# A 3x3 depthwise convolution divided anew between TensorE and VectorE, in a kernel whose instruction order is planned

## The chip, the core and the metric

The kernel runs on one core of one Trainium2 chip. The metric is device time in microseconds (us) from the first to the last instruction with the little that lies around it; the time of the kernel before is the median of three runs. The profile is of one execution on that core.

## The reference, cut to what matters

The input is 32 images of 96 channels and 56x56 pixels, in float32. Each image goes through three parts, and the change is in the first.

```python
# part 1, the convolution block (32 images)
h = relu(bn(einsum('oc,bchw->bohw', w1, x)))      # 96 -> 576 channels
h = relu(bn(dwconv3x3(h, wdw)))                   # each channel by itself, 9 taps
x = x + bn(einsum('oc,bchw->bohw', w2, h))        # 576 -> 96 channels
# part 2, a mixer over the 3136 pixels as tokens
t = t + bn(w2 @ irfft(relu(diag * fft(relu(bn(w1 @ ln(t)))) + bias)))
# part 3, a feed-forward block with rounding to fp8 (5,2) and fp16
t = t + q(W2 @ q(relu(q(W1 @ q(ln(t)) + b1))) + b2)
```

The batch norms are folded into weights and biases when the kernel starts. The depthwise convolution of 576 channels is the largest elementwise work: nine multiply-adds for each of 576 x 3136 values of an image.

## The kernel before, in words

**Stages.** An image is cut into two halves of 28 rows (`R`). For every half, `load_half` brings 29 rows of the 96 input channels into one of three `xs` buffers. The 576 hidden channels are four groups of 128 (`k` = 0 to 3, `NK` = 4) and the last 64.

For each of the four groups, `unit(img, s, k)` does this: `expand` multiplies by `w1T` on TensorE into PSUM (L617), ScalarE evicts with bias and relu into `hs` (L627), ScalarE starts the accumulator `acc` with one tap and the bias (L643, `begin`), and VectorE adds seven taps one by one with a multiply-add over 28 rows (L670, `tap`). The ninth tap is a `product` that ScalarE makes (L659) and that a DMA with addition, issued by GpSimd, adds to `acc` (L678). The groups named in `DOUBLE` (`k` = 1 and 3) make two products, so that VectorE has six taps left; the second product is added to the first by another such DMA. At the end ScalarE applies relu to `acc` (L687).

The last 64 channels have no taps on VectorE. `last_channels` puts even and odd rows on the two halves of the 128 partitions (`hl`, evicted at L738 and L742), and TensorE does the nine taps as matmuls with matrices of diagonals (`band`, L755): of a half image, 12 matmuls with a stationary operand of 128x64 and 12 of 64x64. ScalarE evicts the sum with bias and relu (L784, `al`).

`front` then multiplies the 576 channels by `w2T`, pixel rows becoming partitions (L883 for the four groups, L920 for the last 64), adds the input (a transpose in the same accumulation), evicts (L933), and runs the norm and the first part of the mixer. `mid` does the rest of the mixer, for two halves of the spectrum, and `back` the inverse transform and the feed-forward block, for four quarters.

**Order.** Nothing of this is emitted in the order in which it is written. Every piece is a `step` with an engine, an estimated cost, what it comes after, buffers that it takes and gives, and a rank. `Plan.emit` plays the steps through and gives each engine, whenever it is idle in that play, the ready step of lowest rank. Work of several images so stands interleaved on each engine, and each engine runs its own list strictly in order. Where TensorE has little to do in that play, the planner places `filler` matmuls (L1491), which compute nothing that is used.

**PSUM** is three buffers of two banks for everything (`ps`), and one of two banks for the accumulation of `front` (`pw`), in which the filler also has a corner.

Of the kernel before, what the change touches and what calls it, by code (L numbers as in the profile page):

```python
# [41 lines left out]
C = 96  # L42
# [12 lines left out]
NK = 4  # L55
G = 7
# [71 lines left out]
START = {"last": 9, "front": 7, "mid": 62, "back": 98}  # L128
PACE = {"last": 3.023, "front": 0.4, "mid": 0.54, "back": 0.45}
# [6 lines left out]
SPARSE = 0.75  # L136
FILLER = 0.23
FIRST = 15.0
# [4 lines left out]
DOUBLE = (1, 3)  # L143
# [15 lines left out]
class Plan:  # L159
# [12 lines left out]
    def __init__(self, free):  # L172
        self.free = dict(free)
        self.steps = []
        self.now = self.pace = 0.0
        self.window, self.share, self.slow = 0, {}, False
        self.moving = 0.0
        self.filler, self.recent = None, []
# [20 lines left out]
    def sparse(self, now):  # L199

        self.recent = [r for r in self.recent if r[1] > now - self.WINDOW]
        return sum(b - max(a, now - self.WINDOW) for a, b in self.recent) < SPARSE * self.WINDOW

# [10 lines left out]
    def step(self, engine, cost, emit, after=(), take=(), give=(), late=None, rank=None):  # L214
        late = self.LATE.get(engine, 0.1) if late is None else late
        if rank is None:
            rank = self.now
            self.now += self.pace
        s = Step(engine, cost, emit, list(after), list(take), list(give), late, rank, len(self.steps))
        self.steps.append(s)  # L220
        return s

    def emit(self):
# [6 lines left out]
        work = sum(s.engine == "PE" for s in self.steps)  # L230
        while events:
# [12 lines left out]
            for engine, heap in ready.items():  # L244
# [3 lines left out]
                while heap:  # L248
# [13 lines left out]
                    if engine == "PE":  # L262
                        self.recent.append((now, now + cost))
                        work -= 1
# [7 lines left out]
                if engine == "PE" and idle[engine] and work and now > FIRST and self.sparse(now):  # L272

                    self.filler()
                    idle[engine] = False
                    cost = self.stretched(now, FILLER)
                    self.recent.append((now, now + cost))
                    heapq.heappush(events, (now + cost, count, engine, None))
                    count += 1
# [4 lines left out]
def tile_kernel(ctx: ExitStack, tc: tile.TileContext, d: dict, out: bass.AP):  # L284
# [5 lines left out]
    psa = ctx.enter_context(tc.tile_pool(name="psa", bufs=3, space=PSUM))  # L290
    psw = ctx.enter_context(tc.tile_pool(name="psw", bufs=1, space=PSUM))
    dram = ctx.enter_context(tc.tile_pool(name="scratch", bufs=2, space=DRAM))


    pw = psw.tile([128, 2, 512], F32, name="pw", tag="pw")
# [25 lines left out]
    w1T = cst([C, HD], "w1T")  # L321
# [12 lines left out]
    b1 = cst([128, NK + 1], "b1")  # L334
# [10 lines left out]
    band = cst([128, 2, 3, 128], "band")  # L345
    gd = cst([KD, G, C], "gd")
    xnT = cst([C + 1, G, 128], "xnT")
    xs_ring = [cst([C, XW], f"xs{j}") for j in range(3)]


    hl = [cst([128, RP + 1, S], f"hl{s}") for s in range(2)]


    scratch = [w1.tile([128, G * SK], F32, name="eo", tag="brief", bufs=8) for _ in range(3)]
    scratch += [w1.tile([128, G * SK], F32, name="V", tag="brief", bufs=8) for _ in range(2)]
# [26 lines left out]
    load(nc.sync, w1T, d["w1T"])  # L382
# [5 lines left out]
    nc.gpsimd.memset(band, 0.0)  # L388
    nc.gpsimd.memset(hl[0][0:64, 0, :], 0.0)
    nc.gpsimd.memset(hl[1][64:128, RP, :], 0.0)  # L390
    nc.gpsimd.memset(ones, 1.0)

    def loads():
# [3 lines left out]
        for s in range(2):  # L397
            load(q, w2T[64 * s : 64 * s + 64, NK, :], d["w2T"][NK * 128 :, :])
        yield rows
# [46 lines left out]
    for k in range(NK + 1):  # L446
# [7 lines left out]
        )  # L454
    shift_of(b1, vec[:, 1, :], vec[:, 2, :], s, tmp(128, NK + 1))
    nc.vector.tensor_mul(w1T[:, 0:512], w1T[:, 0:512], ps[0:C, 0, :])
    nc.vector.tensor_mul(w1T[:, 512:HD], w1T[:, 512:HD], ps[0:C, 1, 0 : HD - 512])
# [5 lines left out]
    def bands(j):  # L463
        def f():

            for dc in range(3):
                for i in range(2):
                    for o in range(2):
                        dr = 2 * j - 1 + i - o
                        if abs(dr) <= 1:  # L470
                            at, to = slice(64 * i, 64 * i + 64), slice(64 * o, 64 * o + 64)
                            k = 3 * (dr + 1) + dc
                            nc.vector.tensor_scalar_mul(band[at, j, dc, to], ident[at, at], wdw[at, NK, k : k + 1])

        return f

    def second():
# [11 lines left out]
        nc.vector.tensor_mul(w2T, w2T, s.unsqueeze(1).to_broadcast([128, NK + 1, C]))  # L489

# [38 lines left out]
    def ffn():  # L529
# [6 lines left out]
        for o, v, p, n in ((b1q, fb, 128, 3), (b2q, fc, C, 1)):  # L536
# [11 lines left out]
            "ps": 3, "pw": 1, "hs": 3, "acc": 7, "product": 3, "hl0": 1, "hl1": 1, "al": 2,  # L548
            "xt": 1, "norma": 2, "brief": 8, "xnT": 1, "z": 2, "ya": 1, "wb": 1, "yb": 2,
# [21 lines left out]
    bands_set = [step("DVE", 1.2, bands(j), rank=2.0 + j) for j in range(2)]  # L571
    sets = []
    for n, (f, count) in enumerate(((second, 7), (attention, 6), (mixer, 21), (ffn, 4))):
        t = step("SP", 0.55 * count, fetch, sets[-1:], late=(150e3, HARD), rank=-20.0 + n)
        sets.append(step("DVE", 3.0, f, sets[-1:] + [t], rank=14.0 + 4 * n))
    second_set, mixer_set, *mid_set = sets

    def spare(name, p, n):

        t = w1.tile([128, R, S], F32, name=name, bufs={"acc": 7, "product": 3}[name])  # L580
# [5 lines left out]
    def load_half(img, s):  # L586
# [8 lines left out]
        if n >= 3:  # L595
            i, t = divmod(n - 3, 2)
            after = [taken[i, t], strips[i, t, "hl"]]
        loaded[img, s] = step("SP", 0.1, load, after, late=read(C * XW), rank=16 * n - 24)

    def unit(img, s, k):  # L600
        n = (2 * img + s) * NK + k
        o = R * s - base[s]
        up = 1 - 2 * s
# [6 lines left out]
        def expand(h):  # L610
            def mm():
                if h == 0:
                    u["hs"] = w2.tile([128, XR, S], F32, name="hs", bufs=3)
                u[h] = psum()
                for j in range(2):
# [4 lines left out]
                        rhs=xs[img, s][0:C, at : at + QW],  # L620
# [4 lines left out]
            def evict():  # L625
                flat = u["hs"].rearrange("p r c -> p (r c)")
                nc.scalar.activation(  # L627
                    flat[:, 2 * h * QW : 2 * (h + 1) * QW].rearrange("p (j w) -> p j w", j=2),
                    u[h][:, :, 0:QW],
                    AF.Relu,  # L630
                    bias=b1[:, k : k + 1],
                )

            after = [loaded[img, s]] if h == 0 else [u["first"]]
            e = u["first"] = step("PE", pe(QW, 128, 4), mm, after, ["ps"] + ["hs"] * (h == 0), rank=4 * n + OFF[0] + h)
            return step("ACT", act(2 * QW, 1), evict, [e], [], ["ps"], rank=4 * n + OFF[0] + h)

        e = [expand(0), expand(1)]

        def begin():  # L640

            acc[img, s, k] = w1.tile([128, R, S], F32, name="acc", bufs=7)
            nc.scalar.activation(  # L643
                acc[img, s, k],
                u["hs"][:, o + up : o + up + R, :],
# [5 lines left out]
        def span(dr, dc):  # L651

            return max(0, -(o + dr)), min(R, XR - o - dr), max(0, -dc), S - max(0, dc)

        def product(dr):
            def f():
                ra, rb, _, _ = span(dr, 0)
                u["p", dr] = w1.tile([128, R, S], F32, name="product", bufs=3)
                nc.scalar.activation(  # L659
                    u["p", dr][:, ra:rb, :], u["hs"][:, ra + o + dr : rb + o + dr, :], AF.Copy, scale=weight(dr, 0)  # L660
# [4 lines left out]
        def tap(dr, dc):  # L665
            def f():
                ra, rb, ca, cb = span(dr, dc)
                src = u["hs"][:, ra + o + dr : rb + o + dr, ca + dc : cb + dc]
                dst = acc[img, s, k][:, ra:rb, ca:cb]
                nc.vector.scalar_tensor_tensor(dst, src, weight(dr, dc), dst, ALU.mult, ALU.add)  # L670
# [888 lines left out]
```

## Time and profile before

| | |
|---|---|
| median of three runs | 4469.97 us (4468.09 to 4476.27) |
| profiled execution, span | 4469.5 us |
| TensorE: matmul records, busy | 34916, 98% of the span |
| VectorE: instructions, busy | 7053, 96% |
| ScalarE: instructions, busy | 5390, 92% |
| DMA engines, mean busy in the steady part | 75% |
| one image in the steady part | 134.6 us |

The time of the profiled execution is its span, 4469.5 us, and the fraction of a microsecond around it; it stands within 0.5 us of the median. The lines of the profile give, for a group of instructions, the line of the kernel, the engine, the operation, `out<-in` by the program's names, the shapes, the count, the summed busy time and the mean duration in nanoseconds, and behind a bar the idle time of the engine ahead of it and what ended it. A float32 matmul leaves two records in the trace, so that counts of TensorE's records are twice those of the program. Records of TensorE [...]overlap: the time that a run of matmuls really takes is read from the start of the run to the start of the next one, in the timeline.

### The profile page before, as it was taken

The numbers are of one execution on the slowest core, as the hardware profiler recorded it, in microseconds if no ns is written. First come the engines' busy times: TensorE is split into PE (matmuls) and PEld (weight loads), VectorE is DVE, ScalarE is ACT, GpSimd is POOL, SyncE is SP. The second block draws the span as 40 slices with busy tenths as digits, with TensorE's granted clock in tenths as the row PEclk, the third lists the DMA queues.
The fourth block names the chain that finished last, engine by engine and source line by source line (L and its number), as shares of the span: only waits on it lengthen the run. The fifth ranks groups of instructions, "written<-read, shape, count | busy, mean of one in ns | idle before, by whom it ended". The sixth has DMA issues, their size and how long they took to land.

```text
span 4469.5 us, 87997 instructions
## 1 busy us (share of the span) xinstructions
PE 4366.5 (98%) x34916; PEld 3248.3 (73%) x34916; DVE 4307.1 (96%) x7053; ACT 4103.5 (92%) x5390; POOL 339.6 (8%) x403
## 2 busy tenths in 40 slices
PE   8999999999999999999999999999999999999998
PEld 5767777777777777777777777777777777777777
DVE  8999999999999999999999999999999999999977
ACT  5778999999999999999999999999999999999975
POOL 1100000000000000000000000000000000000000
PEclk9999999999999999999999999999999999999999
DMA  5667777777777777777777777777777777777763
GB/s 106 144 147 174 192 172 184 189 176 183 192 171 188 187 176 184 189 176 184 187 173 191 187 174 188 182 176 192 184 176 188 176 180 194 180 177 191 169 180 107
DMA packets 390992, 789.43 MB, mean 177 GB/s; under 512 B 135696, under 2 KB 236628, under 8 KB 390580
## 3 DMA queue, kind: packets, MB, share of 16 engines
q1 hardware_dynamic: 335028, 479.15, 38.1%
q0 software_dynamic: 55488, 304.64, 34.2%
q8 instruction: 275, 4.51, 0.4%
q14 instruction: 137, 1.12, 0.1%
q10 hardware_dynamic: 64, 0.01, 0.0%
HBM read 286.38 MB, written 192.68 MB: 107 GB/s over the span
## 4 chain that ended last, share of the span: by engine, by line
PE 37%; DVE 32%; ACT 15%; issue 3%; DMA 3%; ACTq 0%; DVEq 0%; POOLq 0%; SPq 0%
DVE acc L670 20%; PE pw L883 10%; PE ps L617 5%; PE ps L1005 3%; PE ps L1036 3%; PE ps L1123 3%; PE ps L1329 2%; ACT h L1395 2%; DVE sb L1152 2%; DVE V L1152 2%; DMA acc<-product 2%; ACT product L659 1%; ACT hs L627 1%; PE ps L755 1%; PE ps L1447 1%
## 5 line engine op out<-in xcount | busy, mean ns | idle before, releaser
L670 DVE SCALAR_TENSOR_TENSOR acc<-hs,wdw,acc 128x1540 f32<-128x1540 f32 (+2 forms) x1664 | 2970.5, 1795 | 5.9 <-ACT acc L643 0.3
L617 PE MATMUL ps<-xs,w1T 96*128 96x406 f32 x2048 | 808.9, 517 | 27.2 <-ACT al L784 12.9
L883 PE MATMUL pw<-w2T,acc 128*112 128x96 f32 x7168 | 788.6, 264 | 3.8 <-ACT acc L687 3.7
L883 PEld LDWEIGHTS pw<-w2T,acc 128*112 128x112 f32 x7168 | 750.5, 179 | 57.5 <-issue 34.6
L659 ACT ACTIVATE product<-hs,wdw 128x1568 f32<-128x1568 f32 (+1 forms) x384 | 610.8, 1599 | 15.2 <-DMA product<-product 15.0
L617 PEld LDWEIGHTS ps<-xs,w1T 96*128 96x128 f32 x2048 | 355.6, 190 | 291.5 <-issue 165.1
L627 ACT ACTIVATE hs<-ps,b 128x812 f32<-128x812 f32 x512 | 481.3, 940 | 84.4 <-PE ps L617 79.5
L678 POOL DMA_DIRECT2D acc<-product x256 | 223.3, 872 | 3709.6 <-DVE df L855 687.2
L643 ACT ACTIVATE acc<-hs,bd,wdw 128x1568 f32<-128x1568 f32 x256 | 436.9, 1707 | 0.2
L755 PE MATMUL ps<-hl,band 128*64 128x385 f32 (+3 forms) x3072 | 418.7, 497 | 4.8 <-ACT hs L627 4.8
L687 ACT ACTIVATE acc<-acc 128x1568 f32<-128x1568 f32 x256 | 388.0, 1516 | 26.1 <-DMA acc<-product 19.9
L1005 PEld LDWEIGHTS ps<-watt,xnT 97*120 97x120 f32 x1792 | 293.2, 182 | 97.3 <-issue 40.8
L1005 PE MATMUL ps<-watt,xnT 97*120 97x192 f32 x1792 | 339.1, 330 | 19.8 <-DVE V L1152 14.7
L1123 PEld LDWEIGHTS ps<-wb,yb 112*128 112x128 f32 x3528 | 297.0, 164 | 48.1 <-issue 35.8
L1410 ACT ACTIVATE h<-h 128x784 fp8e5<-128x784 f16 x348 | 300.2, 863 | 34.4 <-DVE h L1401 34.3
L1395 ACT ACTIVATE h<-ps 128x784 f16<-128x784 f32 x384 | 317.0, 828 | 12.3 <-PE ps L1383 11.5
L1350 ACT ACTIVATE u<-tt,mf,rf 112x96 fp8e5<-112x96 f32 x812 | 317.0, 465 | 0.7
L1123 PE MATMUL ps<-wb,yb 112*128 112x112 f32 x3528 | 317.2, 269 | 0.0
L755 PEld LDWEIGHTS ps<-hl,band 128*64 128x64 f32 (+1 forms) x3072 | 152.7, 135 | 203.0 <-issue 163.4
L1401 DVE TENSOR_SCALAR h<-h,b1q 128x784 f16<-128x784 f16 x384 | 162.3, 423 | 88.9 <-ACT h L1395 88.8
L1036 PE MATMUL ps<-z,wa 56*64 56x384 f32 (+1 forms) x2048 | 223.9, 498 | 1.7 <-ACT hs L627 1.7
L1329 PE MATMUL ps<-gd,wd 114*112 114x96 f32 x1792 | 200.2, 264 | 2.3 <-DMA gd<-gdr 2.0
(171 smaller groups left out, 6621.3 us busy)
## 6 DMA issues: line engine op xcount, KB each, us to landing
acc<-product POOLq DMA_DIRECT2D x256, 784.0 KB, 8.7
product<-product POOLq DMA_DIRECT2D x128, 756.0 KB, 11.2
yb<-ydr SPq DMA_DIRECT2D x252, 294.0 KB
wd<-in_wd_dram SPq DMA_DIRECT2D x128, 349.1 KB
wb<-in_wb_dram SPq DMA_DIRECT2D x63, 686.0 KB
ydr<-ya SPq DMA_DIRECT2D x256, 168.0 KB
xs<-in_x_dram SPq DMA_DIRECT2D x64, 609.0 KB
tdr<-xt SPq DMA_DIRECT2D x64, 588.0 KB
```

The costliest lines, as they stand in the source:

```text
L617: nc.tensor.matmul(u[h][:, j, 0:QW], lhsT=w1T[:, 128 * k : 128 * (k + 1)], rhs=xs[img, s][0:C, at : at + QW], start=True, stop=True,)
L627: nc.scalar.activation(flat[:, 2 * h * QW : 2 * (h + 1) * QW].rearrange("p (j w) -> p j w", j=2), u[h][:, :, 0:QW], AF.Relu, bias=b1[:, k ...
L643: nc.scalar.activation(acc[img, s, k], u["hs"][:, o + up : o + up + R, :], AF.Identity, scale=weight(up, 0), bias=bd[:, k : k + 1],)
L659: nc.scalar.activation(u["p", dr][:, ra:rb, :], u["hs"][:, ra + o + dr : rb + o + dr, :], AF.Copy, scale=weight(dr, 0))
L670: nc.vector.scalar_tensor_tensor(dst, src, weight(dr, dc), dst, ALU.mult, ALU.add)
L687: nc.scalar.activation(acc[img, s, k], acc[img, s, k], AF.Relu)
L755: nc.tensor.matmul(pv[:, :, ca:cb], lhsT=band[rows, j, dc + 1, 64 * o : 64 * o + 64], rhs=H[rows, q : q + 7, ca + dc : cb + dc], skip_grou ...
L883: nc.tensor.matmul(u["pw"][0:SK, t, n % 4, 0:C], lhsT=src[rows, (G * t + n) * SK : (G * t + n + 1) * SK], rhs=rhs, skip_group_check=True, **k,
L1005: nc.tensor.matmul(pv[0:PK, q - a, 0:HA], lhsT=xnT[:, q, 0:PK], rhs=watt, start=True, stop=True,)
L1036: nc.tensor.matmul(u["y", b][64 * c : 64 * c + n, j, 0 : 2 * HA], lhsT=wa[at, 0:n], rhs=rhs, start=True, stop=True)
L1123: nc.tensor.matmul(o, lhsT=lhsT, rhs=u["wb"][:, G * s + q, :], start=True, stop=True)
L1395: nc.scalar.activation(u["h", c].rearrange("p (j w) -> p j w", j=2), u["H", c][:, :, 0:n], AF.Copy)
```

## The change

**Channels 384 to 511** (`k` = 3, now `QK`) leave VectorE. A new function `quads` expands them as before, and does the nine taps on TensorE: the array is used as sixteen tiles of 32x32. A half image is four windows of seven rows; for each tap there are sixteen matmuls, one for each pair of a block of 32 input channels and a window, each with a 32x32 diagonal (`wq`) as stationary operand and seven rows as moving operand. Window `t` of channel block `i` goes to output partitions `32*((i + t) % 4)` of a bank that belongs to the window, so the channels stand rotated by window, and `w2r`, `bdr` are rotated copies of weights and bias. The nine taps are three steps, the two PSUM buffers are held over all three, and ScalarE evicts them with four activations into `q_ring`.

**The last 64 channels** leave TensorE's taps. They become one `unit` for the whole image ("pair"): the two image halves lie on the two halves of the 128 partitions, even and odd rows interleaved by window, so that the taps of both are done by VectorE in instructions of the same size as those of the other groups. Two short matmuls with zeros (`nought`) fill the row beyond the image's edge.

**The rest.** `front` takes three groups from `w2T`, the rotated one from `w2r` (one more matmul per 128 columns where a tile of 112 pixels crosses two windows), and the last 64 from the pair. The bias of `expand` becomes a row of `w1T` against a row of ones in `xs`, so evictions apply relu alone. `filler` and the buffer `pw` are gone, and PSUM is four equal buffers. There are two `product` buffers in place of three. `DOUBLE` names the units (0, 1), "pair" and (1, 1). A table `NUDGE` adds a number to the rank of each step of an image.

```diff
+HS, ACCS, PRODUCTS, BRIEFS = 3, 7, 2, 8
+UNIT = 32 / 7
+ORDER = {(0, 0): 0, (0, 1): 1, (0, 2): 2, "pair": 3, (1, 0): 4, (1, 1): 5, (1, 2): 6}
+NUDGE = (-7.64, 3.75, 0.79, ...)
-DOUBLE = (1, 3)
+DOUBLE = ((0, 1), "pair", (1, 1))
...
+        if self.place is not None:
+            rank += NUDGE[self.place] if self.place < len(NUDGE) else 0.0
+            self.place += 1
...
-    psa = ctx.enter_context(tc.tile_pool(name="psa", bufs=3, space=PSUM))
-    psw = ctx.enter_context(tc.tile_pool(name="psw", bufs=1, space=PSUM))
+    psa = ctx.enter_context(tc.tile_pool(name="psa", bufs=4, space=PSUM))
...
-    def last_channels(img, s):
+    def quads(img, s):
...
+        def taps(first):
+            def f():
+                if first == 0:
+                    for n in range(2):
+                        u["d", n] = psum()
+                for dr, dc in TAPS[first : first + 3]:
+                    at = 3 * (dr + 1) + dc + 1
+                    ca, cb = max(0, -dc), S - max(0, dc)
+                    for j in range(4):
+                        for i in range(4):
+                            t = (j - i) % 4
+                            row = 7 * t + R * s - base[s] + dr
+                            ra, rb = max(0, -row), min(7, XR - row)
+                            pv = u["d", t // 2][32 * j : 32 * j + 32, t % 2, 0 : 7 * S].rearrange("p (r c) -> p r c", c=S)
+                            nc.tensor.matmul(
+                                pv[:, ra:rb, ca:cb],
+                                lhsT=wq[32 * i : 32 * i + 32, at, :],
+                                rhs=u["hs"][32 * i : 32 * i + 32, row + ra : row + rb, ca + dc : cb + dc],
+                                start=(dr == 0 and dc == 0),
+                                stop=(dr, dc) == TAPS[-1],
+                                skip_group_check=True,
+                            )
...
+                for b in range(2):
+                    at = 15 * t + 8 * b
+                    nc.scalar.activation(
+                        q_ring[n % 2][:, at : at + 7, :].rearrange("p r c -> p (r c)"),
+                        u["d", t][:, b, 0 : 7 * S],
+                        AF.Relu,
+                        bias=bdr[:, 2 * t + b : 2 * t + b + 1],
+                    )
...
-                    for k in range(NK):
+                    for k in range(QK):
...
+                    src = acc[img, (s, QK)].rearrange("p (t r) c -> p t (r c)", t=2)[:, t, :]
+                    for b in (0,) if i < 3 else (1,) if i > 3 else (0, 1):
+                        at = (2 * i + b) * S
+                        nc.tensor.matmul(
+                            u["pw", i // 4][0:SK, t, i % 4, 0:C],
+                            lhsT=src[:, at : at + SK],
+                            rhs=w2r[:, 2 * t + b, :],
...
     for i in range(nimg):
+        plan.place = 0
         for s in range(2):
             load_half(i, s)
-            last_channels(i, s)
-            for k in range(NK):
-                unit(i, s, k)
+        for s in range(2):
+            quads(i, s)
+        for what in ORDER:
+            unit(i, what)
+        for s in range(2):
             front(i, s)
```

Counted over the program, VectorE's taps go from 1664 instructions to 1472, the accumulating DMAs from 384 to 320, and TensorE's depthwise matmuls from 1536 to 9216.

## The prediction

> **What bounds the kernel now.** I read the busy shares first, then the stretches (is there a steady part, and how long is one image?), then the groups by form, and last TensorE's timeline, since its busy share is no measure.
>
> ```profile
> PE 4366.5 (98%) x34916; PEld 3248.3 (73%) x34916; DVE 4307.1 (96%) x7053; ACT 4103.5 (92%) x5390; POOL 339.6 (8%) x403
> ```
>
> Three engines look full. Two neighbouring stretches of 134.6 us (columns: stretch, length, then busy time of PE, PEld, DVE, ACT, POOL) hold the same work:
>
> ```profile
> 2000.00:2134.60 134.60, 133.16 (x1072) 98.39 (x1072) 132.26 (x215) 129.41 (x173) 10.40 (x12) 1.00 0.75 183
> 2134.60:2269.20 134.60, 132.91 (x1069) 98.18 (x1069) 132.18 (x215) 129.15 (x172) 10.41 (x12) 1.00 0.75 182
> ```
>
> So one image takes 134.6 us, and 32 of them 4307; the other 162 us of the span are the start and the end. VectorE is idle for 2.4 us of an image (1.8%): it is the bound. ScalarE needs 129.3. [...]I took its need from the timeline of 26 images (538 to 4038 us): for each kind of run (line, length, whether the next one uses the array in tiles) the fastest fifth of the times from its start to the next run's start counts as work, what others take beyond as waiting. Work comes to 130.1 us an image. In it are the filler matmuls (the stretch, their busy time and records):
>
> ```profile
> 538.40:4038.00 3499.60, 66.44 (x416) 57.66 (x416) 1.00 0.75 183
> ```
>
> A pair of their records lasts 0.22 us start to start, longer ahead of a change of mode: 2.1 us an image. **TensorE's own need is 128.0 us**, close under VectorE's. That is the number on which this prediction rests.
>
> [...]The trace shows two and four tiles at once; sixteen no run here shows:
>
> ```profile
> 2038.63 2.17 PE L755 MATMUL ps<-hl,band 128*64 128x392 f32 x12
> 2040.73 1.63 PE L617 MATMUL ps<-xs,w1T 96*128 96x406 f32 x4
> ...
> 2047.07 2.18 PE L755 MATMUL ps<-hl,band 64*64 64x392 f32 x24
> 2049.18 0.88 PE L987 MATMUL ps<-ident,xn 112*96 112x112 f32 x7
> ```
>
> Twelve records two at a time (six rounds) take 2.10 us to the next run; twenty-four, four at a time, 2.11. Doubling the tiles at equal rounds costs 0.01 us. [...]with bias 917 ns, without 828, both of 784 elements (L738, L1395 below). [...]sixteen L883 records take 1.56 us ahead of L617 and 1.65 to 1.74 ahead of the tiled L920. In the program's order the changes of mode are 44.4 an image before and 44.6 after, so this costs nothing new.
>
> **The change part by part.** Forms (count, then busy us and mean ns):
>
> ```profile
> L670 DVE SCALAR_TENSOR_TENSOR acc<-hs,wdw,acc 128x1540 f32<-128x1540 f32 x1024 | 1856.5, 1815 | 3.3
> L670 DVE SCALAR_TENSOR_TENSOR acc<-hs,wdw,acc 128x1485 f32<-128x1485 f32 x512 | 899.5, 1758 | 1.5 <-ACT acc L643 0.3
> L738 ACT ACTIVATE hl<-ps,b 128x784 f32<-128x784 f32 x64 | 58.7, 917 | 2.7 <-PE ps L719 2.7
> L1395 ACT ACTIVATE h<-ps 128x784 f16<-128x784 f32 x384 | 317.0, 828 | 12.3 <-PE ps L1383 11.5 <-DVE h L1408 0.4 <-ACT h L1395 0.2
> ```
>
> *VectorE.* 1540-element taps fall from 1024 to 960, 1485-element ones from 512 to 384: 64 x 1.815 + 128 x 1.758 = 341 us, 10.7 an image. The pair's taps have the same forms and price. Need: 132.2 - 10.7 = **121.5**.
>
> *ScalarE.* Expansion evictions: 512 at 0.940 become 512 at 0.851 (no bias): -45.6. The last channels' evictions and finish (58.7 + 19.5 + 58.6) go: -136.8. The pair's 64 evictions of 896 elements at 0.92: +58.9. Four evictions of 392 for each half, with bias, at 0.917 - 392 x 0.00083 = 0.59: 256 x 0.59 = +151. 32 fewer `begin` (1.707), 64 fewer short products (1.564), 32 fewer relus (1.516): -203. Sum -176 us, 5.5 an image. Need: **123.8**.
>
> *TensorE.* Taps: a step has three taps, so 96 records in six rounds of sixteen: 2.11 us[...], 2.18. Six steps an image are 13.1 against 12.6: +0.5. `front`: 28 fewer L883 matmuls an image and 32 new ones of the same form, at 2 x 0.098: +0.8. The pair's expansion streams 448 columns where 392 were, against two fewer short matmuls, and the zeros: +0.2. Filler: gone. Need: 128.0 + 1.5 = **129.5**.
>
> *DMA and queues.* GpSimd issues 320 accumulating DMAs, not 384; the engines were 75% busy, so this lies beside other work and is counted at nothing. What queued behind them on GpSimd's queue moves up. Two `product` buffers, not three: ScalarE can be held until a DMA (8.7 to 11.2 us to landing) has read one, and what is queued behind it are evictions for TensorE. Before, this wait was 15 us in all; with seven units an image, 18.8 us apart, I take it as unchanged, and its worst case is in the second rival. At the start: seven more loads on SP ahead of the attention weights, seven small DMAs on GpSimd, five matmuls and two copies for the bias row, against the 18 `band` instructions: between -3 and +12 us, I take +5.
>
> *Sum.* The bound moves from VectorE to TensorE. VectorE reached 98.2% of its bound; TensorE has two neighbours at 92 and 94% and fewer waits on VectorE, so I take 98.5%: 129.5 / 0.985 = 131.5 us an image. 32 x 131.5 = 4208, plus 162 and 5: **4375 us**, against the profiled execution's own 4469.5 (its span; the median of the runs is within 0.5 of it). The gain is 3 us an image although VectorE loses 10.7: the rest goes into TensorE's limit.
>
> **The rivals.**
>
> *TensorE's work is overstated (faster).* What I count as work may hold waits that every run of a kind had because VectorE was late. If half the difference to the bare stream (126.8 with the additions: 0.84 ns for each column and record of a round, or 0.88 for each weight column where that is more) goes, the need is 128.1, at 99% 129.4 an image: 4308; all of it gives about 4265. For it: filler was placed, so there were holes. Against: weight loads of a next run that can't start early are real.
>
> *PSUM turnover and order eat the gain (no change, either side).* The taps hold two of four PSUM buffers over three steps, at least 6.5 us plus two evictions, `front` holds one more; then a single buffer serves all else, and each turn of it waits for an eviction of about 0.85 us on a ScalarE at 94%, or one held by a product. Four such waits an image are 3.4 us, the gain. 133 to 136 us an image: 4420 to 4520. Without filler there is also nothing to keep the clock up in long holes. Against it: `front` no longer waits for its only buffer.
>
> *The sixteen tiles do not run at once (slower).* The place is the six tap steps of an image. If weight loads or the reads of one row block by four tiles make two turns of every round, a tap takes 1.35 us, not 0.73: 18 x 0.62 = 11.2 us more, TensorE needs 140.7, at 98.5% 142.8 an image, 4740 us. It decides from 0.90 us a tap on, where the 3.1 us an image are used up. From the other side, 0.65 us (rounds of 0.323[...]) would gain 1.4 an image. For it: no line here shows more than four tiles, and 144 matmuls a half image, each with its weight load, stand where 24 were. Against: four cost what two cost.
>
> That the change does not do what it says is excluded by the order: the counts above are those of its instructions.
>
> **How the numbers follow.** Main case (4330 to 4420) 0.43, TensorE overstated 0.25, order and PSUM 0.18, tiles in turns 0.14. The measurement can tell about 0.2% from no change (4461 to 4479 is "same"). Order and PSUM I split 0.07 faster, 0.04 same, 0.07 slower. Faster: 0.43 + 0.25 + 0.07 = 0.75; same 0.04; slower 0.07 + 0.14 = 0.21. The range from 4265 to 4490 holds the main case, nearly all of the faster one and most of the third: 0.82.
>
> **What would show it.** Right: one image of 130 to 133 us; VectorE busy for 92 to 93% of the steady part, and no longer the engine without gaps; 1472 taps at the old price; a run of 48 tap matmuls (96 records) at 2.1 to 2.3 us from its start to the next; evictions without bias near 0.85 us; no waits of TensorE above a few us an image. Wrong: such a run at 2.6 us or more (tiles), PSUM waits of TensorE ended by evictions that add to over 3 us an image (turnover), a clock below 1.00 in the steady part, or VectorE still at 98%, which would mean that its taps grew dearer.

## The result, and the profile after

The kernel after takes 4525.18 us (median of 4 runs, 4518.04 to 4529.23) against 4471.23 for the kernel before in the same comparison: a ratio of 1.012 (95% interval 1.0105 to 1.0134), 54 us slower. The profiled span is 4523.7 us. Forecast were 4375 and a gain.

The engines' busy shares, from the page of the kernel after:

```profile
PE 4388.9 (97%) x49370; PEld 3305.8 (73%) x49370; DVE 4044.0 (89%) x6850; ACT 3954.0 (87%) x5390; POOL 291.8 (6%) x349
```

VectorE and ScalarE fell as forecast (96% to 89%, 92% to 87%); TensorE has 14454 matmul records more. The chain of work that ended last has moved to TensorE; the pages before and after give its shares of the span:

```profile
PE 37%; DVE 32%; ACT 15%; issue 3%; DMA 3%; ACTq 0%; DVEq 0%; POOLq 0%; SPq 0%
```

```profile
PE 87%; ACT 4%; DMA 4%; issue 3%; DVE 3%; SPq 0%; ACTq 0%; DVEq 0%; POOLq 0%
```

Now three neighbouring stretches, each one image long (columns as before: stretch, length, busy time of PE, PEld, DVE, ACT, POOL, then clock, DMA share, GB/s):

```profile
2475.20:2609.30 134.10, 134.03 (x1542) 101.51 (x1538) 124.04 (x209) 125.02 (x173) 8.70 (x10) 1.00 0.71 173
2609.30:2745.70 136.40, 135.21 (x1548) 101.87 (x1544) 124.29 (x209) 125.03 (x174) 8.70 (x10) 1.00 0.70 169
2745.70:2887.00 141.30, 139.76 (x1656) 104.31 (x1654) 127.30 (x212) 124.99 (x173) 8.72 (x10) 1.00 0.68 168
```

Before, the two stretches shown were 134.6 us each; now they differ by 7 us at nearly the same work. I measured every image, by the distance of one ScalarE eviction (`uT`, L1476; `uT`'s counterpart L1366 before) from the same one in the next image. Before, images 5 to 28 take 134.6 to 135.2 us, mean 134.7. After, the regular ones take 134.3 to 134.5, others up to 141.9, and the mean is 136.4. 32 times that difference of 1.73 us is 55 us, the whole loss; start and end together (span less 32 mean images) are 159.8 before and 158.6 after. So two questions are left: why is a *regular* image no shorter than before, and what makes the others long?

The groups by form of the kernel after that answer to the priced ones:

```profile
L753 DVE SCALAR_TENSOR_TENSOR acc<-hs,wdw,acc 128x1540 f32<-128x1540 f32 x960 | 1735.2, 1815 | 100.0 <-ACT acc L725 98.5
L753 DVE SCALAR_TENSOR_TENSOR acc<-hs,wdw,acc 128x1485 f32<-128x1485 f32 x384 | 671.7, 1757 | 21.0 <-ACT acc L725 17.9
L666 ACT ACTIVATE hs<-ps 128x812 f32<-128x812 f32 x384 | 326.5, 852 | 55.4 <-PE ps L656 48.1 <-DVE acc L753 4.4 <-issue 2.8
L869 ACT ACTIVATE q<-ps,bdr 128x392 f32<-128x392 f32 x256 | 129.7, 587 | 108.8 <-PE ps L853 108.8
L776 ACT ACTIVATE acc<-acc 128x1568 f32<-128x1568 f32 x32 | 48.1, 1504 | 32.3 <-DMA acc<-product 32.3
```

Counts and prices are those of the forecast: 1815 and 1757 ns for the taps, 852 for an eviction without bias (0.851 forecast), 587 for the quarter evictions (0.59). VectorE now idles ahead of its taps. The last row is new: the relu of the pair (L776), one an image, is held 32.3 us by the DMA that adds its product.

TensorE's timeline after, in a regular image (start, busy time, operation, records):

```profile
1929.66 2.79 PE L853 MATMUL ps<-hs,wq 32*32 32x392 f32 x96
1932.38 1.56 PE L1224 MATMUL ps<-wb,yb 112*64 112x112 f32 x28
1933.88 1.63 PE L656 MATMUL ps<-xs,w1T 97*128 97x406 f32 x4
1935.44 2.77 PE L853 MATMUL ps<-hs,wq 32*32 32x385 f32 x96
1938.14 1.20 PE L1538 MATMUL ps<-h,w2q 128*96 128x392 fp8e5 x6
```

From start to start a tap step takes 1932.38 - 1929.66 = 2.72 us and 1938.14 - 1935.44 = 2.70, that is **0.90 us a tap**, where 2.18 us and 0.73 were forecast. Five of an image's six steps take 2.69 to 2.72 us and one, ahead of L1086, 3.03; together they are 16.6 us, not 13.1. The 0.90 is just where the prediction put the point from which its tile rival decides, and a step is over its sign of being wrong (2.6 us).

And the same place in a long image of the kernel after:

```profile
1112.29 2.77 PE L853 MATMUL ps<-hs,wq 32*32 32x385 f32 x96
...
1114.34 1.51 ACT L776 ACTIVATE acc<-acc 128x1568 f32<-128x1568 f32 x1 [4.16 <-DMA acc<-product]
...
1116.88 0.84 ACT L666 ACTIVATE hs<-ps 128x812 f32<-128x812 f32 x1
...
1117.77 1.56 PE L1538 MATMUL ps<-h,w2q 128*96 128x392 fp8e5 x6 [2.70 <-ACT hs L666]
1119.25 3.92 PE L853 MATMUL ps<-hs,wq 32*32 32x385 f32 x96
```

The relu waits 4.16 us for its DMA. Behind it on ScalarE stands the eviction L666, which gives a PSUM buffer back; L1538 waits 2.70 us for that. The next tap step then takes 3.92 us, since the granted clock is half of the full one ("half clock" below) for 3.4 us from 1118.4. In the regular image the relu starts 7.3 us after its DMA is issued and just makes it; here it is 10.5 us.

### The profile page after: what moved, and what is told of

Same layout as the page of the kernel before. It is cut to its first block, busy times and chain, and to the rows that moved or that the text cites. A ratio compares the mean times of both kernels' runs of the same rounds, so it can differ in the third digit from the quotient of the medians.

```text
span 4523.7 us, 116600 instructions
## 1 busy us (share of the span) xinstructions
PE 4388.9 (97%) x49370; PEld 3305.8 (73%) x49370; DVE 4044.0 (89%) x6850; ACT 3954.0 (87%) x5390; POOL 291.8 (6%) x349
## 4 chain that ended last, share of the span: by engine, by line
PE 87%; ACT 4%; DMA 4%; issue 3%; DVE 3%; SPq 0%; ACTq 0%; DVEq 0%; POOLq 0%
PE ps L970 13%; PE ps L656 11%; PE ps L853 11%; PE ps L1104 7%; PE ps L1224 6%; PE ps L1005 4%; PE ps L1439 4%; PE ps L1323 4%; PE ps L1538 3%; PE ps L1135 3%; PE ps L815 3%; PE ps L1493 3%; PE ps L1019 2%; PE ps L1311 2%; PE ps L684 2%
## 5 line engine op out<-in xcount | busy, mean ns | idle before, releaser
L753 DVE SCALAR_TENSOR_TENSOR acc<-hs,wdw,acc 128x1540 f32<-128x1540 f32 (+2 forms) x1472 | 2630.3, 1797 | 122.1 <-ACT acc L725 116.5
L970 PE MATMUL ps<-w2T,acc 128*112 128x96 f32 x5376 | 688.6, 265 | 0.0
L970 PEld LDWEIGHTS ps<-w2T,acc 128*112 128x112 f32 x5376 | 616.2, 179 | 41.7 <-issue 24.9
L656 PE MATMUL ps<-xs,w1T 97*128 97x406 f32 x1536 | 598.5, 513 | 1.3 <-issue 0.8
L853 PE MATMUL ps<-hs,wq 32*32 32x392 f32 (+3 forms) x18432 | 561.2, 496 | 21.5 <-issue 14.0
L853 PEld LDWEIGHTS ps<-hs,wq 32*32 32x32 f32 x18432 | 289.2, 104 | 235.5 <-issue 113.0
L656 PEld LDWEIGHTS ps<-xs,w1T 97*128 97x128 f32 x1536 | 275.8, 191 | 180.9 <-issue 102.0
L666 ACT ACTIVATE hs<-ps 128x812 f32<-128x812 f32 x384 | 326.5, 852 | 55.4 <-PE ps L656 48.1
L1005 PE MATMUL ps<-w2r,q 128*112 128x96 f32 x2048 | 349.5, 263 | 0.0
L1005 PEld LDWEIGHTS ps<-w2r,q 128*112 128x112 f32 x2048 | 274.6, 179 | 0.0
```

The lines of the kernel that those rows point to most:

```text
L656: nc.tensor.matmul(u[h][:, j, 0:QW], lhsT=w1T[:, 128 * k : 128 * (k + 1)], rhs=xs[img, s][:, at : at + QW], start=True, stop=True,)
L666: nc.scalar.activation(flat[:, 2 * h * QW : 2 * (h + 1) * QW].rearrange("p (j w) -> p j w", j=2), u[h][:, :, 0:QW], AF.Relu)
L753: nc.vector.scalar_tensor_tensor(dst, source(dr, ra, rb, ca + dc, cb + dc), weight(dr, dc), dst, ALU.mult, ALU.add)
L853: nc.tensor.matmul(pv[:, ra:rb, ca:cb], lhsT=wq[32 * i : 32 * i + 32, at, :], rhs=u["hs"][32 * i : 32 * i + 32, row + ra : row + rb, ca + ...
L970: nc.tensor.matmul(u["pw", n // 4][0:SK, t, n % 4, 0:C], lhsT=src[rows, (G * t + n) * SK : (G * t + n + 1) * SK], rhs=rhs, skip_group_chec ...
L1005: nc.tensor.matmul(u["pw", i // 4][0:SK, t, i % 4, 0:C], lhsT=src[:, at : at + SK], rhs=w2r[:, 2 * t + b, :], start=False, stop=False, ski ...
```

## The experiments

All ratios are to the kernel before on the same chip.

**What a tap step costs.** Two rival readings: W, the weights of the next tap are not loaded until the tiles of the tap before it are done, so that a step follows the rows and tiles of a tap; L, weight loads in turn, so that it follows their number alone.

`half_rows`: all taps but the first stream four rows of seven.

```diff
-ra, rb = max(0, -row), min(7, XR - row)
+ra, rb = max(0, -row), min(7 if (dr, dc) == (0, 0) else 4, XR - row)
```

> The changed kernel with its order of steps, but eight of the nine taps on TensorE stream at most four of the seven rows of a window (those rows' sums are left out of the result). Equal count of matmuls and weight loads. Theory W ([...]the weights of the next tap can't be loaded early): a step of three taps falls from 2.70 us to about 1.75 (2.0 for the one with the full tap), TensorE's work by 5.3 us an image, the time to 4360-4420. Rival L (weight loads of 32 columns pass one by one at 28 ns, 96 of them 2.70 us): the step stays at 2.7 and the time within 15 us of 4524.

Measured: a tap step 1.88 us at its fastest, median 2.21, where the kernel after has 2.70 with as many loads; 4479.48 us, 1.0024 (1.0013 to 1.0035). Serial loads, which do not depend on the rows, are refuted. The shortest image is 130.3 us, but the mean 135.0.

`twelve`: all taps but the first leave out one block of 32 channels.

```diff
-for i in range(4):
+for i in range(4 if (dr, dc) == (0, 0) else 3):
```

> The changed kernel with its order, but eight of the nine taps leave out the fourth block of 32 input channels: twelve tiles at once[...], not sixteen; those sums are left out of the result. W: a step of three taps 2.35-2.45 us[...]; time 4450-4490. L: 72 to 80 loads at 28 ns, 2.05-2.2 us; time 4400-4440. Bare stream: 1.95.

Measured: 2.49 to 2.51 us for 72 records; 4471.90, 1.000 (0.9988 to 1.0012), images 133.3 with a mean of 134.3. Above both expectations, nearer to W. Taken together, time follows rows and tiles only in part: four rows of seven in eight of nine taps took it from 2.70 to 1.88, twelve tiles of sixteen to 2.50.

The two runs also show what a tap step is worth. The six steps of an image add to 16.6 us in the kernel after, 15.5 in `twelve` and 12.4 in the shortest image of `half_rows`; the shortest images take 134.4, 133.3 and 130.3 us. So the image falls by 1.1 and 4.1 us for 1.1 and 4.2 us of tap steps: in a regular image of the kernel after, TensorE's time goes into the image whole.

The raw records of one step of the kernel after fit W too. The first tap's sixteen tiles start 6.7 ns apart. At the next tap, tile 0 loads its weights at once (2005.465 us), but tile 1 only at 2005.975, just after the first matmul's second pass has ended (2005.945), and from there on the tiles start some 16.5 ns apart. So fifteen of the sixteen tiles load late, behind the tap before. What holds their loads there was not shown.

`fp16`: channels 384 to 511 and their diagonals in fp16, one pass in place of two (48 records a step, not 96).

```diff
-wq = cst([128, 9, 32], "wq")
+wq = cst([128, 9, 32], "wq", F16)
... (u["hs"] of these channels in F16 as well)
```

> The changed kernel with its order, but the expanded channels 384-511 and the 32x32 diagonals are in fp16: one pass per matmul, not two (other rounding of these 128 channels). Theory W with TensorE as the bound: a step 1.1-1.25 us, TensorE's work 9 us an image less, the bound then ScalarE and the order: 4250-4340. Rival O (the order of steps and the waits between engines set the time, TensorE's length of taps does not): 4440-4520.

Measured: 4429.42, 0.990 (0.9881 to 0.992). A step takes 0.75 us at its fastest, 2 us less, and 1.13 at the median; there are six an image. The mean image falls by 3.4 us to 133.0, the shortest to 130.4. TensorE has half the clock for 215 us of the steady part (540 to 4040 us).

**Order and filler.** `no_table` sets the rank table to zeros; `before_no_filler` takes the filler from the kernel before; `after_fill` puts 210 filler matmuls into both ends of the kernel after.

```diff
-NUDGE = (-7.64, 3.75, ...)
+NUDGE = ()
```
```diff
-if engine == "PE" and idle[engine] and work and now > FIRST and self.sparse(now):
+if False:
```
```diff
+if engine == "PE" and now > 15:
+    for _ in range(min(8, int((now - self.ended) / 0.3))):
+        if self.free["ps"]:
+            self.filler()
```

> The changed kernel with all numbers of the rank table at zero: another order, the same instructions. If the table was what costs (rival O: an order found for step costs that the chip does not keep), 4430-4500, faster than with it. W with TensorE as the bound: not below 4460; without the table's fitting more waits, 4530-4700.

> The kernel before without its filler matmuls, and so with an order planned anew by the same planner; the same result. Theory C (without filler TensorE's clock halves more often, and each us at half clock costs up to half a us where TensorE is late): 15 to 60 us slower than before, 4485-4530, with over 100 us at half clock against 53. Rival: filler is worth nothing while VectorE is the bound: within 10 us of 4470.

> The changed kernel in its order, with 210 filler matmuls put where the plan leaves TensorE idle, nearly all in the first 500 and last 200 us; the same result. Theory C: half-clock time at the two ends falls from 137 us towards 60, 4490-4515. If the ends wait on chains of other engines anyway: 4515-4535.

Measured: 4913.57, 1.099 (1.0971 to 1.1011); 4623.31, 1.034 (1.0325 to 1.0356), mean image 140.0, 102 us of half clock in the steady part where before there was none; 4519.36, 1.0115 (1.0098 to 1.0132). So the order is worth 390 us and the filler, with the order that goes with it, 150; the prediction counted removed filler as a gain of 2.1 us an image. `after_fill` can't be told from the kernel after (the intervals overlap), though half clock outside the steady part fell from 137 to 72 us: no gain from the clock at the ends shows.

**Is VectorE the bound?** `before_fewer` and `after_fewer` leave one VectorE tap out of every unit.

```diff
 def f():
+    if (dr, dc) == (0, 1):
+        return
     ra, rb, ca, cb = span(dr, dc)
```

> The kernel before in its order, but each unit leaves out one of VectorE's taps (that tap is missing in the sums): VectorE has 14.4 us an image less. It measures where the next limit lies when VectorE is relieved and TensorE gets nothing for it. By the prediction's numbers TensorE's 130.1 with filler and ScalarE's 129.3 hold an image at 131-133 us: 4370-4420. If TensorE's need was overstated: 4290-4350. If VectorE was not the bound: 4455-4475.

> The changed kernel in its order, but each unit leaves out one of VectorE's taps (missing in the sums): VectorE has 12.6 us an image less. Theory W (TensorE is the bound): no more than 15 us faster than 4524. Rival V (VectorE's chain of taps still sets when things come free): 40 us or more faster, below 4485.

Measured: 4463.98, 0.9983 (0.9977 to 0.999), and 4519.94, 1.0113 (1.0098 to 1.0128). In the kernel before VectorE loses 14.4 us of 132 an image, and the image 0.05; in the kernel after 12.6, and the mean image 0.3. It was no bound, in either kernel.

**Then TensorE, or ScalarE?** In the kernel before, `before_fp16` puts the last 64 channels' taps into fp16, `before_both` adds the VectorE relief, `before_more` issues four expansion matmuls an image twice, `before_less` leaves out 14 small `w2T` matmuls, `before_act` halves the rows of the last relu; `fp16_fewer` takes VectorE taps from `fp16`.

```diff
-band = cst([128, 2, 3, 128], "band")
+band = cst([128, 2, 3, 128], "band", F16)
... (hl in F16 as well)
```
```diff
-for j in range(2):
+for j in (0, 0, 1) if (s, h) == (0, 0) else range(2):
```
```diff
 for k in range(NK):
+    if (k, t) == (1, 1):
+        continue
```
```diff
-nc.scalar.activation(acc[img, s, k], acc[img, s, k], AF.Relu)
+nc.scalar.activation(acc[img, s, k][:, 0:14, :], acc[img, s, k][:, 0:14, :], AF.Relu)
```

> The kernel before with the expanded last 64 channels and the diagonals of band in fp16: TensorE's nine taps run in one pass, about 6 us less of its 130.1 us an image; the plan and VectorE are untouched. If TensorE was what set the 134.6 us an image (theory after before_fewer): what it gives back is limited by VectorE's 132.2 us, so about 1.5 to 3 us an image, 4375 to 4425 us, and waits of TensorE on ScalarE appear. If VectorE was the bound: no gain, 4460 to 4472. If the planned order itself, with waits that change engine all the time, holds each engine: -5 to -20, 4450 to 4465.

> The kernel before with both reliefs: fp16 taps on TensorE (-6 us an image) and one VectorE tap less in every unit (-14.4 us an image; those sums miss a tap). VectorE alone gave 7 us of the program. If TensorE was the bound and VectorE the next one close behind it: now ScalarE at 129.3 us an image is next, 4300 to 4370, and clearly more than before_fp16 alone gives. If the order holds everything: within 20 us of before_fp16.

> The kernel before with four extra 406-column expansion matmuls an image (the first of each group of the upper half is issued twice, its result overwritten by itself): about 2.7 us more work for TensorE an image, 87 us over the program, plan and all else as before. If TensorE was the bound: +70 to +100, 4540 to 4570. If TensorE had the slack that the prediction gave it (130.1 against 134.6): +0 to +15. Half and half, +30 to +50, if only part of the steps lies on the path that sets the end.

> The kernel before with the second of the four groups left out of w2T for every second tile of 112 pixels (those sums lack 128 channels): 14 matmuls an image of 2 x 98 ns, 2.7 us less for TensorE, in pieces of 0.2 us, so without holes; before_more added as much. If TensorE's work sets the time in both directions: -55 to -85, 4385 to 4415. If what is taken away turns into waits for ScalarE or VectorE: -0 to -20, 4450 to 4470.

> The kernel before with the last relu of each group on half the rows only (the other half keeps its negative values): 8 x 0.75 us, some 6 us less for ScalarE an image, nothing else changed. If ScalarE's place in the order is what holds TensorE: -40 to -130, 4340 to 4430. If TensorE alone sets the time: -0 to -15, 4455 to 4470.

> The kernel after with fp16 taps of channels 384 to 511 (4429 us alone) and one VectorE tap less in every unit of the other channels (-12.6 us an image of VectorE, which alone gave 5 us; those sums miss a tap). If TensorE alone sets the time of the kernel after: no more than 10 us below fp16, 4415 to 4430. If VectorE is next behind TensorE (it was busy for 91% in fp16): 4330 to 4400.

| run | us | ratio, interval | image, mean and shortest |
|---|---|---|---|
| before_fp16 | 4515.05 | 1.0104 (1.0087 to 1.0121) | 136.1, 134.3 |
| before_both | 4501.36 | 1.0067 (1.0052 to 1.0082) | 136.0, 134.1 |
| before_more | 4538.01 | 1.0152 (1.0137 to 1.0167) | 136.75, 136.7 |
| before_less | 4460.99 | 0.9975 (0.9965 to 0.9984) | 134.3, 134.1 |
| before_act | 4446.65 | 0.9945 (0.993 to 0.996) | 134.0, 133.9 |
| fp16_fewer | 4423.52 | 0.9889 (0.9865 to 0.9913) | 133.5, 130.0 |

TensorE's work acts one way. 2.7 us more cost 2.1; 2.7 us less give 0.4; and 6 us less of ScalarE give 0.6. Nothing taken from one engine shortens the image by as much as half a per cent: engine orders are fixed, three engines are nearly full, and what one gains waits for the next. Which chain holds 134 us when one engine is relieved is not settled.

`before_fp16` shows more than that: less work made the kernel *slower*. TensorE's timeline in it:

```profile
2060.88 0.69 PE L755 MATMUL ps<-hl,band 64*64 64x392 f16 x12
2064.51 1.54 PE L987 MATMUL ps<-ident,xn 112*96 112x112 f32 x7 [2.94 <-ACT y L1437]
2065.84 2.55 PE L617 MATMUL ps<-xs,w1T 96*128 96x406 f32 x4
```

and the stretches around it (PE's busy time is the first number after the length, its clock the first after POOL):

```profile
2061.10:2064.50 3.40, 0.47 (x12) 0.09 (x4) 3.40 (x5) 3.40 (x6) 0.27 (x1) 0.99 0.14 49
2064.50:2067.90 3.40, 3.39 (x11) 2.38 (x12) 3.40 (x6) 2.58 (x6) 0.59 (x1) 0.50 0.73 148
```

The taps end early, TensorE then waits 2.94 us for an eviction, busy for 0.47 us of 3.4, and the clock is halved in the next 3.4 (0.50): L987 takes 1.54 us where the kernel before has 0.88. This happens in 47 places of the steady part, 224 us at half clock in all; that costs up to half of it, 4.4 us an image, more than the 1.5 to 3 us that were to be gained. Without it the mean image would be about 131.7 (an estimate: 136.1 - 4.4).

**What makes images long?** `after_no_dma` drops the DMAs that add the products.

```diff
-nc.gpsimd.dma_start(out=..., in_=..., accum_op=ALU.add)
+return
```

> The kernel after without the accumulating DMAs: ScalarE makes the products, nothing adds them (those sums miss one or two taps), so no product buffer is ever held by a DMA (10 waits, 28.6 us in the steady part, each followed by TensorE waiting and by half clock). If these waits make the slow images: an image of 134.4 to 134.8 us throughout, no half clock in the steady part, 4465 to 4490. If the slow images come from the tap steps or from DMA traffic of other kinds: 4505 to 4525.

Measured: 4458.15, 0.9967 (0.9954 to 0.998), 67 us less than the kernel after. Its images are 134.4 us, at most 135.0, and TensorE has one wait in the steady part (engine, line, releaser; us in all, times, longest):

```profile
PE ps L1099 <- issue: 0.5, 1, 0.5
```

So without these DMAs there are no long images, and TensorE, which hardly waits, sets the 134.4 us. `after_later` asks which of their effects. It leaves all DMAs and moves one instruction an image: the pair's relu is issued four ScalarE steps later, behind the evictions that it held up.

```diff
... (in words: issued earlier where a step that needs it comes first)
+if s in self.later:
+    self.held = [s, 4]
+else:
     s.emit()
+    if self.held and engine == "ACT":
+        self.held[1] -= 1
+        if not self.held[1]:
+            self.held[0].emit()
+            self.held = None
```

> The kernel after with one instruction an image moved: the relu of the pair is issued on ScalarE four steps later (behind V, hs, product and y), about 6.5 us, with all DMAs as they were. If the wait of this relu for its DMA (12 waits, 32 us) makes the slow images: the wait goes, an image of 133.5 to 134.6 us without half clock in the steady part, 4440 to 4475 us, 50 to 85 us less than the kernel after. If DMA traffic as such slows things: 4500 to 4525.

Measured: 4505.11, 1.0076 (1.0063 to 1.0088): 20 us less than the kernel after, not 50 to 85. The wait of the relu is gone, yet the mean image is 135.8. Each image runs the same 161 runs of matmuls, so I compared every run's time with the same run in a regular image: the excess now lies in and after the tap steps. The worst, in TensorE's timeline of `after_later` (its L868 is L853 of the kernel after):

```profile
2940.43 2.60 PE L868 MATMUL ps<-hs,wq 32*32 32x385 f32 x75
2945.58 1.03 PE L868 MATMUL ps<-hs,wq 32*32 32x385 f32 x21 [2.55 <-issue]
2946.54 2.92 PE L1119 MATMUL ps<-watt,xnT 97*120 97x192 f32 x8
```

TensorE stops inside a tap step, after 75 of 96 records, with no wait that the profile can name ("issue"). The place fits the packets of one DMA queue, which the profile calls "instruction". Of the steady part, before and then after (queue, kind: packets, MB, share of 16 engines):

```profile
q8 instruction: 219, 3.59, 0.4%
```

```profile
q8 instruction: 310, 5.08, 0.6%
```

Their count goes with TensorE's instructions: over the program 275 packets of 16 KB before and 388 after, which is 254 of TensorE's loads and matmuls for each packet in both kernels, and about 256 with the few records of its sequencer; I take the packets for those instructions. A tap step has 192 of them in 2.7 us, and packets follow one another within 5 us in 50 places after, in none before (the smallest distance there is 6.1 us). In the stop above the next packet starts at 2943.09, 0.54 us after the last instruction, and lands at 2944.21; TensorE goes on 1.37 us later. I counted all stops of TensorE over 0.9 us in the steady part (from the start of one matmul to the start of the next), and those that end 1.2 to 1.8 us after such a packet has landed; the last column counts the stops for which the profile names no releaser ("issue"):

| run | stops | of these after a packet | us | "issue" |
|---|---|---|---|---|
| before | 0 | 0 | 0 | 0 |
| after | 18 | 13 | 21.5 | 10 |
| after_later | 12 | 12 | 21.6 | 11 |
| after_no_dma (same TensorE program, DMA engines 40% busy, not 70%) | 0 | 0 | 0 | 0 |
| twelve (a quarter fewer tap instructions) | 5 | 0 | 0 | 0 |
| half_rows (same instructions in 1.9 to 2.2 us) | 34 | 25 | 50.8 | 24 |

With a packet every 11 us, one stop in twenty would end in that span of 0.6 us by chance. Two of the 13 in the kernel after stand at L1538, where the profile names the eviction, so they show nothing of the packets. But every "issue" stop ends in the span, and all of them, with 55 more in `fp16_zeros` below, come at the same place of a packet: 193 instructions above a multiple of 256, counted from the start of the program, 100 times out of 100. The stops with a named releaser lie at many places. By the table, stops come where instructions are used fastest (192 in 2.7 us and less) and go where the DMA engines are freer (40% busy) or the instructions a quarter fewer. That TensorE has run out of instructions there and waits for the packet, and that the packet is held up behind the adding DMAs' packets, is my reading of this and was not shown; the packet's own transfer takes as long with them as without (median 1.07 and 1.10 us), so the delay would lie ahead of its start.

`fp16_zeros` was to hold the clock in `fp16` with three taps of zeros in every step.

```diff
-for dr, dc in TAPS[first : first + 3]:
# in words
+for dr, dc, at in [first tap] + [(0, 0, 9)] * 3 + [other two]:   # slot 9 of wq is zero
```

> The kernel fp16 with three more taps of zeros in every tap step, whose products change nothing: about 0.8 us more for each step, 4.9 us of useless TensorE work an image, 156 us over the program, mostly ahead of the places at which fp16 waits (2.3 to 3 us) and then has half the clock (215 us of it in the steady part). If the half clock after holes eats the gain: half-clock time in the steady part falls under 60 us, an image from 133.0 to 130 to 132, 4340 to 4410 us, faster than fp16 in spite of more work. If TensorE's work is what counts: +100 to +150, 4530 to 4580. If both cancel, or order alone holds: 4420 to 4450.

Measured: 4507.85, 1.0069 (1.0049 to 1.009). Half clock fell only from 215 to 148 us, and TensorE stops 60 times after such a packet, 120 us in all; 55 of these stops, 111 us, have no other releaser. These steps use 192 instructions in 1.3 us at the fastest.

`fp16_later` is `fp16` with the edit of `after_later`: half the tap instructions, and the relu out of the way.

> The kernel fp16 with the relu of the pair moved in the same way. In fp16 TensorE waits in nearly every image for the eviction behind that relu (L1540 <- hs L666, 90 us in 28 waits), with half the clock after it. If the relu's place makes these holes: that wait falls under 30 us, half-clock time in the steady part from 215 to under 100 us, 4350 to 4400 us. If the holes come from TensorE being ahead of everything: 4410 to 4430.

Measured: **4380.46, 0.9797 (0.9784 to 0.9809)**, 2% faster than the kernel before and, by the medians, 3% faster than the one after, at the price of rounding these channels and their weights to fp16. TensorE's longest waits in `fp16` and then in `fp16_later`:

```profile
PE ps L1540 <- ACT hs L666: 87.3, 27, 7.9
```

```profile
PE ps L1241 <- DMA yb<-ydr: 67.8, 20, 5.6
PE ps L1574 <- DVE V L1270: 25.6, 27, 1.0
PE ps L1555 <- ACT hs L679: 25.5, 27, 0.9
```

The wait behind the relu (L1540, now L1555) falls from 7.9 us at the longest to 0.9, half clock in the steady part from 215 to 133 us (under 100 were expected), the mean image from 133.0 to 131.4.

## Why the prediction was wrong, point by point

- **"VectorE ... is the bound": wrong.** Fullness was taken for a bound. Taking 14.4 us from it gave 0.05 us an image (`before_fewer`). The step built on it, that TensorE then comes to 98.5% of its own need, had nothing to stand on.
- **The tap step: the term mis-sized most.** "six rounds of sixteen", 2.18 us, was the author's estimate: the 2.11 us that runs of four tiles took, and 0.07 for twelve more starts, which stand 6 to 7 ns apart in those runs. That sixteen tiles go as four do was shown by no trace of the kernel before. It measured 2.70, and the six steps 16.6 us an image against 13.1. `twelve` and `half_rows` show that this goes into a regular image one for one. With it the sum gives (129.5 + 3.5) / 0.985 = 135.0, and the regular image is 134.4. The third rival had named place and threshold (0.90 us), with two turns as the mechanism; what the records of the one step followed above show instead is one turn in which fifteen of the sixteen tiles load late, and then start 16.5 ns apart, not 6.7.
- **"TensorE's own need is 128.0 us": too low, and the sum near by luck.** These are TensorE's waits in the steady part of the kernel before (line, releaser: us in all, times, longest), as far as the profile shows them; two smaller groups add 0.5 us:

```profile
PE ps L1005 <- DVE V L1152: 12.5, 26, 0.5
PE ps L617 <- ACT al L784: 12.0, 52, 0.2
PE ps L617 <- ACT h L1395: 8.3, 27, 0.4
```

  They come to 33 us in 26 images, 1.3 an image; taking the fastest fifth of each kind of run as work had left 4.5 as waiting. `before_more` agrees: of 2.7 us more work, 2.1 lengthened the image. Most of that "waiting" was thus TensorE's own time. The 1.5% that the sum then added for waits covered for it: in `after_no_dma` TensorE waits for 0.5 us in 26 images, and they still take 134.4 us each.
- **"Filler: gone", 2.1 us gained: wrong in kind.** `before_no_filler` (+3.4%) and `before_fp16` (less work, +1%), with 102 and 224 us of half clock in the steady part where before there was none, show that useless work at the right place keeps the clock; the kernel after has 20 us of half clock in its steady part.
- **"counted at nothing" for the adding DMAs: wrong.** Fewer they are, but with them the kernel is 67 us slower than without, the mean image 2.0 us longer. The prediction looked for their wait at the product buffers and took it as unchanged; it came at the pair's relu, which is ordered 7.3 us behind its DMA, and in the ten "issue" stops of TensorE that ended just after a packet of the queue "instruction" had landed, which no step counted. By an estimate from the trace, the evictions' waits (17.6 us), the ten "issue" stops (14.4) and half of the 20.5 us at half clock (10.2) make 42 of the some 52 us by which 26 images exceed 26 regular ones; the rest is not assigned.
- **The second rival, PSUM and order**, gave 4420 to 4520 and came nearest in time (4525); its mechanism, a PSUM turn behind a ScalarE held by a product's DMA, is what L1538 shows, in six images of the steady part (17.6 us).
- **Right:** VectorE's and ScalarE's counts and prices, 0.85 us evictions. The first rival, TensorE overstated, fell: its work was understated.
- **Less sure than it seemed:** that a change of tiling mode shows in the trace. The sixteen L883 records take 1.65 us ahead of L617, too, in 26 of 52 places of the steady part. Five of the six tap steps end in such a change without a cost that shows, and why the sixth takes 0.3 us more stays open. The +5 at the start did not show (start and end 159.8 to 158.6).

In the sum: the gain of 3.1 us an image was used up by the tap's price, to -0.3 us; the long images added 2.0. 32 x 1.7 is the 55 us.

## What to carry to other kernels

Before calling an engine the bound, take work from it on the chip: 98% busy said nothing here, and taking from any one engine of the kernel before gave next to nothing (0.6 us an image at most), while adding to TensorE cost three quarters of what was added. Price an operation that no trace shows by a run of that operation; and where many small instructions replace few large ones, count instructions a microsecond too: here 192 in 2.7 us came with ten stops, 14.4 us of the steady part, for which the profile names no releaser. An instruction that waits for a DMA stands best behind everything on its engine that others wait for: moving one relu an image gave 20 us in one version and 49 in another.

## What the runs showed of the hardware that was not expected

- For each packet of 16 KB on the queue "instruction" there are about 254 loads and matmuls of TensorE (275 and 388 packets). Where 192 were used in 2.7 us beside DMA engines 70% busy, ten stops of 0.9 to 2.1 us without another releaser ended 1.3 to 1.7 us after a packet had landed (after); where 192 were used in 1.3 us, there were 55 in 3500 us (`fp16_zeros`). All 100 stops without another releaser came at the same place of a packet.
- Sixteen float32 tiles take 0.90 us a tap of two passes, where two rounds of four tiles took 0.70 (a third of 2.11 us, before); in one pass (fp16), 0.25 us at the fastest.
- The clock fell to half also after waits under 3 us (2.7 us ahead of 1118.4), each of the six times in the steady part of the kernel after for 3.41 us: stretches in which TensorE was busy for 0.47 us (`before_fp16`, above) or 0.70 us (after, 1115.0 to 1118.4) of 3.4 were enough.
